# Attention row sums: ten of GpSimd's additions of the first diagonal tile replaced by accumulating transfers

## The chip, the cores and the metric

The kernel runs on one core of one Trainium2 chip. The metric is the device time of one execution in microseconds (us). Before the change it is 2240.48 us, the median of 3 runs (2238.31 to 2241.14). The profiled execution, from which every duration below comes, took 2238.97 us by the same clock, and 2237.2 us lie between its first and its last instruction. 0.2% of the time, about what a measurement of this kernel can tell from no change, is 4.5 us.

## The reference

One block of a transformer on two batch rows of 2048 tokens with 512 features: adaptive layer norm, causal attention with 16 heads of 32 features, a projection with a gate, then a feed-forward layer of 2048 hidden features. Everything is float32. The change touches the attention alone:

```python
scores = jnp.einsum('bhqd,bhkd->bhqk', q, k) * scale
causal = jnp.tril(jnp.ones((t, t), bool))
scores = jnp.where(causal, scores, -jnp.inf)
attn = jax.nn.softmax(scores, axis=-1)
out = jnp.einsum('bhqk,bhkd->bhqd', attn, v)
```

The kernel computes the softmax as unnormalised exponentials, their products with the values, and the sums of the exponentials over the keys; the division by the sums comes later, in another stage.

## The kernel before, in words

**Units and steps.** The attention of a batch row (`attention_phase`) goes through 16 units, numbered u = 0 to 15. A unit (c, i) is a chunk c of four heads and a block i of 512 queries; the order of i is 0, 1, 2, 3 for c = 0 and 0, 2, 1, 3 for the other chunks. So units 2, 5, 9 and 13 have i = 2, and units 3, 7, 11 and 15 have i = 3. A unit takes 4i + 3 steps. Each of the first 4i steps handles one tile of 128 keys that all 512 queries see. The last three are diagonal: step 4i, here called **d**, has the first diagonal tile, again 512 queries wide; d+1 packs the second and the fourth diagonal tile together; d+2 has the third. The next unit's steps follow at once, as d+3, d+4 and so on. What a unit leaves over is done by a list of pending work that is flushed at a later step (`flush`).

**One step** (`scores_t`, lines 634 to 696): TensorE writes four PSUM banks, one a head. The first matmuls of a step put the negated row maxima into all four banks (`st<-fold,sel`, line 659), then one matmul a head adds the scores (`st<-qst,kst`, line 668). ScalarE takes the exponential of each bank into an SBUF tile `e` of 128 x 4 x 512 (line 675). There are four such tiles in rotation (`E_BUFS`, line 77), so the exponentials of step n+4 overwrite those of step n. There are four `st` banks, so the first matmuls of a step need the exponentials of the step before to be done with their banks. GpSimd zeroes the masked triangle of the diagonal tiles (`affine_select`, line 687): once for step d, twice for d+1, once for d+2. In the same step TensorE also makes some score products for the maxima of units up to three ahead (`s<-kst,qst`, `row.score`; a bank of the `st` kind may be lent, `st<-kst,qst`).

**Values and sums.** Two steps later (`LAG`) TensorE multiplies `e` with the values into the bank `o` (line 715). The sums over the keys need a matmul with ones as well (`row_sums`, line 836, bank `sm`). To save those matmuls, GpSimd first adds the `e` tiles of four full steps into one tile `ee`, called a chain (lines 698 to 711, recorded at line 700: three additions of 128 x 2048 elements), and TensorE sums the chain once. In units with i of 2 or 3, GpSimd also adds the `e` tile of step d onto the chain of the last group, at step d+1 (line 844), after the three selects of d and d+1. The chain is then summed at the flush of step d+4 (lines 869 and 870), together with the other two diagonal tiles, which TensorE sums directly. `ee` has two buffers (line 78). At the end of a unit ScalarE copies `o` and `sm` into SBUF tiles `ot` and `sums` (lines 737 and 743, two buffers each), and SyncE stores them.

**What orders the work.** The order of the instructions on each engine is the program's own (`keep_in_program_order`, lines 205 to 215). All loads and stores of the attention are issued by SyncE (SP), in order. At the start of unit u it issues the four query loads of unit u+3 (line 780; four tiles in rotation, so they wait until unit u-1 is through with its queries, which is during its step d+2). At the start of units 4 and 8 it also loads the keys of the next chunk (line 783). Unit 12 reads the sums of units 0 to 11 back (`inverses`, line 398).

Of the kernel before, what the change touches and what calls it, by code (L numbers as in the profile page):

```python
# [8 lines left out]
F32 = mybir.dt.float32  # L9
# [3 lines left out]
ALU = mybir.AluOpType  # L13
# [4 lines left out]
P = 128  # L18
# [3 lines left out]
QB = 512  # L22
# [5 lines left out]
def dit_block_kernel(  # L28
# [36 lines left out]
    nc = tc.nc  # L65
# [9 lines left out]
    NG = T // MT  # L75
    LAG = 2
    E_BUFS = 4
    EE_BUFS = 2
    AHEAD = 3

    const = ctx.enter_context(tc.tile_pool(name="const", bufs=1))
# [89 lines left out]
    n_early = (C - 1) * NQ  # L171
# [37 lines left out]
    def act(ins):  # L209

        return tc.keep_in_program_order(ins)
# [412 lines left out]
    def attention_phase(row):  # L624
        b, vv, kst, qst = row.b, row.vv, row.kst, row.qst
        row.paced = True
        with pool(f"att{b}") as ap, pool(
# [70 lines left out]
            def add(u, dst, x, y):  # L698
                if u < len(units) - 1:
                    act(nc.gpsimd.tensor_tensor(dst, x, y, ALU.add))  # L700
                    return
                for h in range(HC):
                    act(nc.vector.tensor_tensor(dst[:, h], x[:, h], y[:, h], ALU.add))

            def add_to(u, chain, es):
                add(u, chain, chain, es)

            def begin_chain(u, es0, es1):
                chain = ap.tile([P, HC, QB], F32, tag="ee", name="ee", bufs=EE_BUFS)
                add(u, chain, es0, es1)  # L710
                return chain

            def products(dst, lhs, es, q0, at, first, last):
                for h in range(HC):
# [2 lines left out]
                        es[:, h, at : at + QB - q0], start=first, stop=last,  # L717
                    )

            def begin_diagonal(es0, es1):  # L720
                chain = ap.tile([P, HC, QB], F32, tag="ee", name="ee", bufs=EE_BUFS)
                act(nc.gpsimd.tensor_copy(chain[:, :, :P], es0[:, :, :P]))
                act(
                    nc.gpsimd.tensor_tensor(
                        chain[:, :, P:], es0[:, :, P:], es1[:, :, : QB - P], ALU.add
                    )
                )
                return chain
# [5 lines left out]
            def finish(u, o):  # L734

                c, i = units[u]
                ot = ap.tile([P, QB], F32, tag="ot", name="ot", bufs=2)
                act(nc.scalar.copy(ot, o))
                nc.sync.dma_start(od[b][i][:, c, :], ot)

            def finish_sums(u, sm):

                sums = ap.tile([P, QB], F32, tag="sums", name="sums", bufs=2)
                act(nc.scalar.copy(sums, sm))
                nc.sync.dma_start(sums_d[b][u], sums[0:P:HD, :])

# [2 lines left out]
            now = 0  # L749

            def flush(upto):
                while pending and pending[0][0] <= upto:
                    pending.pop(0)[1]()
# [25 lines left out]
            for u, (c, i) in enumerate(units):  # L779
                if NQ <= u + AHEAD < len(units):  # L780
                    row.load_queries(u + AHEAD)
                if u % NQ == 0 and c + 1 < C:
                    row.load_keys(c + 1, 0, NG)
                steps = len(steps_of[u])
                for n_step, tiles in enumerate(steps_of[u]):
                    last = n_step == steps - 1
                    if n_step == 0:
                        summed = set()
                        o = ps_op.tile([P, QB], F32, tag="o", name="o")
                        sm = ps_op.tile([P, QB], F32, tag="sm", name="sm")  # L790
                    ready = row.at

                    n = row.count(
                        due(u, starts[u] + n_step) - QB // 2,
                        u + AHEAD - (n_step < 2 and u > 0),
                    )
                    if u == 0 and n_step < LAG:

                        n = max(n, HC)
                    es, rest = scores_t(u, n_step, n)  # L800
                    rest = len(row.todo) - rest
                    make_rows = False
                    if u + 1 < len(units) and row.rows_made == u + 1:
                        if last:
                            row.score(row.count(cum[-1], u + 1))
                    row.settle()
                    if u + 1 < len(units) and row.rows_made == u + 1:
                        make_rows = last or (ready > u + 1 and n_step >= 1)
                    row.inverses(u, n_step)
                    if u == len(units) - 1:  # L810
                        row.prepare(n_step)
                    if make_rows and not last:
                        row.rows(u + 1)
                    flush(now)
                    if make_rows and last:
                        row.rows(u + 1)
                    row.score(max(0, len(row.todo) - rest))
                    row.settle()

                    def tile_by_tile(dst, lhs, es, tiles, first, last):  # L820
                        at = 0
                        for n, (j, q) in enumerate(tiles):
                            products(
                                dst, lambda h: lhs(j, h), es, q, at,
                                first and n == 0, last and n == len(tiles) - 1,
                            )
                            at += QB - q

                    def values(es=es, tiles=tiles, c=c, o=o, first=n_step == 0, last=last):
                        tile_by_tile(  # L830
                            o,
                            lambda j, h: vv[:, j, (c * HC + h) * HD : (c * HC + h + 1) * HD],
                            es, tiles, first, last,
                        )

                    def row_sums(es, last, tiles=((0, 0),), sm=sm, summed=summed):
                        first = not summed
                        summed.add(len(summed))
                        tile_by_tile(sm, lambda j, h: ones[:, :HD], es, tiles, first, last)

                    pending.append((now + LAG, values))
                    sums_of, wait = None, 0
                    if i and n_step == i * TQ + 1:
                        add_to(u, chain, single)
                    if n_step < i * TQ:
                        k = n_step % TQ
                        if k == 0:
                            even = es
                        elif k == 1:
                            chain = begin_chain(u, even, es)  # L850
                        else:
                            add_to(u, chain, es)
                        if k == TQ - 1 and n_step + 1 < i * TQ:
                            sums_of, wait = (chain, False), 2
                    elif i < 2 and u < len(units) - 2:
                        if n_step == i * TQ:
                            single = es
                        elif not last:
                            pair = es
                            if i == 0:  # L860
                                chain = begin_diagonal(single, pair)
                        else:
                            if i:
                                add_tail(chain, pair, P, 0)
                            add_tail(chain, pair, 3 * P, 3 * P)
                            add_tail(chain, es, 2 * P, 0)
                            sums_of, wait = (chain, True), 2
                    elif i and n_step == i * TQ:
                        single = es
                        sums_of, wait = (chain, False), 2  # L870
                    else:

                        sums_of, wait = (es, last, tiles), i > 0 and not last
                    if sums_of:
                        pending.append(
                            (now + LAG + wait, lambda f=row_sums, s=sums_of: f(*s))
                        )
                    if last:
                        pending.append((now + LAG, lambda u=u, o=o: finish(u, o)))
                        pending.append(  # L880
                            (now + LAG + wait, lambda u=u, sm=sm: finish_sums(u, sm))
                        )
                    pending.sort(key=lambda p: p[0])
                    now += 1
# [482 lines left out]
    with pool("wada") as wp, pool("qkv0") as qp, pool("hl0") as hp, pool(  # L1367
# [160 lines left out]
        pieces.done()  # L1528

    attention_phase(row)  # L1530


# [67 lines left out]
    with ExitStack() as mlp:  # L1600
# [7 lines left out]
        sums = [  # L1608
            wp.tile([P, 2 * MT], F32, tag=f"sum{n}", name=f"sum{n}") for n in range(4)
        ]  # L1610
# [926 lines left out]
```

## Time and profile before

| | us |
|---|---|
| median of 3 runs | 2240.48 |
| the profiled execution | 2238.97 |
| its span | 2237.2 |
| TensorE busy in the span | 2196.1 |
| GpSimd busy in the span | 1458.9 |
| attention of the first batch row | about 205 to 715 |
| attention of the second batch row | about 950 to 1455 |

PE is TensorE's matmuls, PEld its weight loads, DVE VectorE, ACT ScalarE, POOL GpSimd and SPq the sequencer that issues SyncE's transfers. A row of the view in order of time has start, duration, engine, line, operation, output and inputs, how many instructions were merged, and in brackets the idle time before it with the instruction that ended it. A row of the windows has for each engine its busy time and number of instructions, then the granted clock of TensorE, the busy share of the 16 DMA engines and the rate that they moved.

### The profile page before, as it was taken

Reading aid. Unit: us, or ns where it says so; the run is one execution under the profiler, and the core shown is the slowest. Engines: PE = TensorE matmul, PEld = TensorE weight load, DVE = VectorE, ACT = ScalarE, POOL = GpSimd, SP = SyncE. Lnnn points to the kernel's source line nnn. Section 1 sums busy time; section 2 is a strip of 40 time slices with the busy share of each in tenths; the row PEclk is TensorE's granted clock in tenths of the full one; section 3 lists DMA queues with packets and bytes.
Section 4 is the critical chain, followed back from the end, with each engine's and each line's share of the span. In section 5 each row is a group of like instructions: output and inputs, shape, how many; then the busy total and the mean of one; then the engine's idle time right before and its main releaser. Section 6 shows DMA issues by size and latency. Waiting matters only on the chain.

```text
span 2237.2 us, 34305 instructions
## 1 busy us (share of the span) xinstructions
PE 2196.1 (98%) x12273; PEld 1470.9 (66%) x12273; DVE 1580.7 (71%) x3373; ACT 1038.0 (46%) x2132; POOL 1458.9 (65%) x903
## 2 busy tenths in 40 slices
PE   7999999999999999999999999999999999999998
PEld 5887555555543588855555555345788888888887
DVE  4578766767757676777677777656586687688587
ACT  4444555655555244355655555703323532532520
POOL 4253998998992696189989898456616616535540
PEclk9999999999999999999999999999999999999999
DMA  8787143232233799542324113376655554654653
GB/s 273 249 278 192 42 89 76 67 86 48 88 111 114 258 311 317 153 105 62 86 67 104 35 52 127 105 243 216 236 181 177 192 173 157 212 183 142 219 158 111
DMA packets 166627, 340.99 MB, mean 152 GB/s; under 512 B 17216, under 2 KB 49516, under 8 KB 164664
## 3 DMA queue, kind: packets, MB, share of 16 engines
q1 hardware_dynamic: 158080, 302.05, 45.0%
q0 software_dynamic: 8000, 36.21, 4.3%
q8 instruction: 97, 1.59, 0.3%
q14 instruction: 74, 0.61, 0.1%
q10 hardware_dynamic: 376, 0.55, 0.1%
HBM read 246.46 MB, written 100.14 MB: 155 GB/s over the span
## 4 chain that ended last, share of the span: by engine, by line
PE 88%; DVE 4%; POOL 3%; DMA 2%; ACT 1%; issue 1%; SPq 0%; DVEq 0%; ACTq 0%; POOLq 0%
PE ps_a L207 23%; PE st L207 18%; PE ps_b L207 14%; PE o L207 10%; PE s L207 9%; PE ps_c L207 4%; PE ps_o L207 4%; PE sm L207 3%; DVE junk L503 1%; POOL ee L700 1%; PE ps_xt L215 1%; ACT e L675 1%; DVE mx L509 1%; PE ps_o L215 1%; POOL wqk L949 0%
## 5 line engine op out<-in xcount | busy, mean ns | idle before, releaser
L675 ACT ACTIVATE e<-st 128x512 f32<-128x512 f32 (+1 forms) x1152 | 574.7, 578 | 363.4 <-PE st L207 317.5
L509 DVE TENSOR_REDUCE mx<-s 128x1 f32<-128x512 f32 x576 | 381.7, 686 | 193.9 <-PE s L207 192.9
L700 POOL TENSOR_TENSOR ee<-ee,e 128x2048 f32<-128x2048 f32 x106 | 485.9, 4584 | 10.2 <-ACT e L675 4.3
L207 PE MATMUL st<-qst,kst 128*128 128x512 f32 (+3 forms) x1280 | 408.8, 386 | 0.0
L207 PE MATMUL s<-kst,qst 128*128 128x512 f32 (+3 forms) x1046 | 380.6, 395 | 6.0 <-DVE mx L509 3.7
L207 PE MATMUL ps_a<-sum,w 128*128 128x256 f32 (+1 forms) x1304 | 335.6, 391 | 3.1 <-DVE sum L1637 2.9
L207 PE MATMUL o<-e,vv 128*32 128x512 f32 (+3 forms) x2560 | 293.2, 537 | 0.3 <-POOL e L687 0.3
L207 PEld LDWEIGHTS st<-qst,kst 128*128 128x128 f32 x1280 | 228.5, 188 | 97.5 <-issue 65.7
L207 PEld LDWEIGHTS ps_a<-sum,w 128*128 128x128 f32 x1304 | 246.2, 190 | 44.3 <-issue 6.6
L503 DVE CUSTOM_DVE_ANT_0 junk<-s,causal 128x128 bf16<-128x128 f32 (+3 forms) x470 | 220.8, 470 | 61.2 <-PE s L207 47.4
L207 PEld LDWEIGHTS s<-kst,qst 128*128 128x128 f32 x1046 | 194.9, 188 | 71.0 <-DVE mx L509 17.0
L700 POOL TENSOR_TENSOR ee<-e 128x2048 f32<-128x2048 f32 x42 | 192.5, 4584 | 43.0 <-ACT e L675 43.0
L207 PE MATMUL ps_b<-sum,w 128*128 128x256 f32 (+1 forms) x744 | 186.8, 382 | 0.0
L2228 POOL TENSOR_TENSOR h<-h,h 128x512 f32<-128x512 f32 x96 | 119.4, 1274 | 69.8 <-DVE h L1734 69.8
L207 PEld LDWEIGHTS <-sel 32*128 32x128 bf16 x1152 | 29.6, 91 | 197.5 <-issue 196.6
L207 PEld LDWEIGHTS ps_b<-sum,w 128*128 128x128 f32 x744 | 140.4, 190 | 22.5 <-issue 2.6
L509 DVE TENSOR_REDUCE mx<-st 128x1 f32<-128x512 f32 x192 | 131.1, 683 | 0.5
L687 POOL TENSOR_SCALAR_AFFINE_SELECT e<-e 128x512 f32<-128x512 f32 x128 | 83.2, 669 | 68.1 <-ACT e L675 68.1
L1799 POOL TENSOR_TENSOR sum<-xm 128x256 f32<-128x256 f32 x22 | 23.2, 1054 | 154.3 <-PE ps_a L207 154.3
L207 PEld LDWEIGHTS o<-e,vv 128*32 128x32 f32 x2560 | 59.1, 108 | 92.3 <-issue 73.2
L207 PE MATMUL st<-fold,sel 32*128 32x512 bf16 (+1 forms) x1152 | 117.7, 372 | 1.4
L1071 POOL TENSOR_TENSOR lo<-lo,hi 128x512 fp32r<-128x512 f32 x32 | 40.7, 1274 | 105.7 <-ACT hi L1069 100.7
(263 smaller groups left out, 3580.4 us busy)
## 6 DMA issues: line engine op xcount, KB each, us to landing
w<-w1x SPq DMA_DIRECT2D x42, 896.0 KB
qst<-q SPq DMA_DIRECT2D x128, 256.0 KB
kst<-k SPq DMA_DIRECT2D x128, 256.0 KB
w<-w2d SPq DMA_DIRECT2D x28, 1024.0 KB
w<-w2d SPq DMA_DIRECT2D x28, 768.0 KB
q<-hi SPq DMA_DIRECT2D x32, 256.0 KB
q<-lo SPq DMA_DIRECT2D x32, 256.0 KB
k<-hi SPq DMA_DIRECT2D x32, 256.0 KB
```

What stands on the lines that cost most here:

```text
L207: return tc.keep_in_program_order(nc.tensor.matmul(*args, **kw))
L215: return tc.keep_in_program_order(nc.tensor.transpose(dst, src, ident[:n, :n]))
L503: nc.vector.tensor_tensor_reduce(junk[:, :w], x, causal[:, QB - w :], 1.0, MASKED, ALU.add, ALU.max, m,)
L509: self.vector(nc.vector.tensor_reduce(m, x, axis=AX.X, op=ALU.max))
L675: act(nc.scalar.activation(e4[:, h, :w], sts[h][:, :w], AF.Exp))
L687: nc.gpsimd.affine_select(d, d, pattern=[[0, HC], [1, P]], compare_op=ALU.is_ge, fill=0.0, base=0, channel_multiplier=-1,)
L700: act(nc.gpsimd.tensor_tensor(dst, x, y, ALU.add))
L1071: engine.tensor_tensor(lo, d, hi.bitcast(F32), ALU.subtract)
L1799: act(engine.tensor_tensor(dst, u, v, ALU.subtract))
L2228: act(engine.tensor_tensor(d[j], d[j], x[j], ALU.add))
```

## The change

In units 2, 3, 5, 7 and 9 of each batch row (`joined`: i of 2 or 3, and u below 11), the `e` tile of step d is no longer added onto the chain by a GpSimd instruction. GpSimd issues one DMA of 128 x 2048 floats instead, from `e` in SBUF onto `ee` in SBUF, with an addition as accumulating operation. It stands at the same place in GpSimd's order. The sum of that chain, and with it the end of the unit's sums and their copy and store, moves from the flush of step d+4 to that of d+6 (`JOIN_LAG`). `ee` gets three buffers, `ot` and `sums` one each. Units 11, 13 and 15 are as before.

```diff
-    EE_BUFS = 2
+    EE_BUFS = 3
+    JOIN_LAG = 2
...
+            def join(chain, es):
+                act(nc.gpsimd.dma_start(chain, es, accum_op=ALU.add))
...
-                ot = ap.tile([P, QB], F32, tag="ot", name="ot", bufs=2)
+                ot = ap.tile([P, QB], F32, tag="ot", name="ot", bufs=1)
...
-                sums = ap.tile([P, QB], F32, tag="sums", name="sums", bufs=2)
+                sums = ap.tile([P, QB], F32, tag="sums", name="sums", bufs=1)
...
+                    joined = i >= 2 and u < n_early - 1
                     if i and n_step == i * TQ + 1:
-                        add_to(u, chain, single)
+                        if joined:
+                            join(chain, single)
+                        else:
+                            add_to(u, chain, single)
...
-                        sums_of, wait = (chain, False), 2
+                        sums_of, wait = (chain, joined), 2 + JOIN_LAG * joined
                     else:
 
-                        sums_of, wait = (es, last, tiles), i > 0 and not last
+                        sums_of, wait = (es, last and not joined, tiles), i > 0 and not last
...
-                            (now + LAG + wait, lambda u=u, sm=sm: finish_sums(u, sm))
+                            (
+                                now + LAG + wait + JOIN_LAG * joined,
+                                lambda u=u, sm=sm: finish_sums(u, sm),
+                            )
```

## The prediction

> **What bounds the kernel now.** The first page says where the whole span goes: TensorE is busy 98% of it, and the chain of work that ended last runs through TensorE for 88% and through GpSimd for 3%. GpSimd has many additions of 4.58 us, and these are what the change takes a few of.
>
> ```profile
> span 2237.2 us, 34305 instructions
> PE 2196.1 (98%) x12273; PEld 1470.9 (66%) x12273; DVE 1580.7 (71%) x3373; ACT 1038.0 (46%) x2132; POOL 1458.9 (65%) x903
> PE 88%; DVE 4%; POOL 3%; DMA 2%; ACT 1%; issue 1%; SPq 0%; DVEq 0%; ACTq 0%; POOLq 0%
> L700 POOL TENSOR_TENSOR ee<-ee,e 128x2048 f32<-128x2048 f32 x106 | 485.9, 4584 | 10.2 <-ACT e L675 4.3
> ```
>
> An average over all stages doesn't say what bounds the attention, so next come the windows of its two rows, and the view of the exponentials' line, which lists what ScalarE waited for.
>
> ```profile
> 200.00:715.00 515.00, 508.65 (x3514) 260.98 (x3513) 371.17 (x900) 305.50 (x610) 439.43 (x170) 1.00 0.33 85
> 945.00:1455.00 510.00, 504.34 (x3476) 259.04 (x3475) 369.45 (x899) 304.31 (x607) 434.51 (x166) 1.00 0.32 85
> ```
>
> ```profile
>   POOL ee L700: 29.7, 22
> ```
>
> In 515 us TensorE idles 6.4 us, and in 510 us it idles 5.7 us. So TensorE alone sets the pace of both stages, at full clock. GpSimd is nearly as full (439 of 515), and ScalarE does wait for it 22 times, 29.7 us in all; but TensorE's own idle time, for all reasons together, is less than half of that in the two rows, so most of it doesn't reach TensorE. Whatever the change frees on GpSimd can give back at most the 12.0 us in which TensorE stands still, and what it makes later costs full price once it reaches TensorE.
>
> **What the change removes.** Ten additions of 4.58 us leave GpSimd. TensorE's instructions stay the same in number: ten groups of `sm<-ee` move two steps later, past matmuls that are done anyway.
>
> What waits for the removed addition? The exponentials of step d+4 overwrite the `e` tile of step d, so they need its last reader to be done. The view in order of time shows unit 2: GpSimd ends three selects and starts the addition at 279.13, and ScalarE starts the exponentials of d+4 as soon as it ends. The other four additions of this batch row follow, then the first exponential of d+4 in unit 5, where ScalarE was released by TensorE and not by GpSimd.
>
> ```profile
> 277.35 1.80 POOL L687 TENSOR_SCALAR_AFFINE_SELECT e<-e 128x512 f32<-128x512 f32 x3
> 279.13 4.57 POOL L700 TENSOR_TENSOR ee<-ee,e 128x2048 f32<-128x2048 f32 x1
> 331.64 4.56 POOL L700 TENSOR_TENSOR ee<-ee,e 128x2048 f32<-128x2048 f32 x1
> 379.85 4.59 POOL L700 TENSOR_TENSOR ee<-ee,e 128x2048 f32<-128x2048 f32 x1
> 462.16 4.58 POOL L700 TENSOR_TENSOR ee<-ee,e 128x2048 f32<-128x2048 f32 x1
> 510.21 4.58 POOL L700 TENSOR_TENSOR ee<-ee,e 128x2048 f32<-128x2048 f32 x1
> ```
>
> ```profile
> 283.73 2.06 ACT L675 ACTIVATE e<-st 128x512 f32<-128x512 f32 x4 [1.47 <-POOL ee L700]
> 386.79 0.60 ACT L675 ACTIVATE e<-st 128x512 f32<-128x512 f32 x1 [1.39 <-PE st L207]
> ```
>
> In the changed kernel the last reader is the transfer, and the exponentials of d+4 wait for its landing. **That is the wait put in place of the one removed**, and its length decides.
>
> **How late the landing may be.** Behind the waiting exponential on ScalarE stand the rest of that step and all that follow; TensorE waits for them when it starts step d+5, since its first matmuls write the four `st` banks that these exponentials free. TensorE's rows in order of time give the end of d+4 in unit 2, then the start of d+5 in all five units:
>
> ```profile
> 285.32 1.06 PE L207 MATMUL sm<-ee,ones 128*32 128x512 f32 x8
> 286.20 1.05 PE L207 MATMUL sm<-e,ones 128*32 128x384 f32 x16
> ...
> 288.04 0.40 PE L207 MATMUL st<-fold,sel 32*128 32x512 bf16 x4
> 339.77 0.29 PE L207 MATMUL st<-fold,sel 32*128 32x256 bf16 x4
> 390.92 0.40 PE L207 MATMUL st<-fold,sel 32*128 32x512 bf16 x4
> 470.36 0.29 PE L207 MATMUL st<-fold,sel 32*128 32x256 bf16 x4
> 521.33 0.40 PE L207 MATMUL st<-fold,sel 32*128 32x512 bf16 x4
> ```
>
> The sum over the chain (286.20 - 285.32 = 0.88 us) leaves d+4, so d+5 can start 0.88 us sooner. Four exponentials take 2.06 us. From the moment at which GpSimd comes to the transfer, the landing may take, without any cost:
>
> - unit 2: 288.04 - 279.13 - 0.88 - 2.06 = 5.97 us
> - unit 3: 339.77 - 331.64 - 2.94 = 5.19 us
> - unit 5: 390.92 - 379.85 - 2.94 = 8.13 us
> - unit 7: 470.36 - 462.16 - 2.94 = 5.26 us
> - unit 9: 521.33 - 510.21 - 2.94 = 8.18 us
>
> These allowances sum to 32.73 us. The second batch row runs the same program; its unit 2 has 1032.82 - 1023.85 = 8.97 where the first has 8.91, so I count the first row twice. What a landing takes beyond its allowance stops TensorE, and TensorE has no slack to win it back.
>
> ```profile
> 1023.85 4.58 POOL L700 TENSOR_TENSOR ee<-ee,e 128x2048 f32<-128x2048 f32 x1
> 1032.82 0.40 PE L207 MATMUL st<-fold,sel 32*128 32x512 bf16 x4
> ```
>
> **How long the landing takes.** No accumulating transfer and none from SBUF to SBUF is in this trace. The nearest rows are GpSimd's plain stores of 896 KB from 128 partitions in the first stage: the issue in order of time, the issues and queue of the window 103 to 112, those of 125 to 143, and the line's summary.
>
> ```profile
> 103.48 0.58 POOL L1274 DMA_DIRECT2D w1d<-kst  x1 [0.30 <-POOL kst L1258]
> ```
>
> ```profile
> q0 software_dynamic: 288, 1.84, 49.6%
> ...
> w1d<-kst POOLq DMA_DIRECT2D x1, 896.0 KB, 3.9
> ```
>
> ```profile
> w1d<-kst POOLq DMA_DIRECT2D x1, 896.0 KB, 9.3
> w1d<-qst POOLq DMA_DIRECT2D x1, 896.0 KB, 9.9
> ```
>
> ```profile
> DMA to landing us min/median/max: 3.9/4.9/9.9
> ```
>
> An issue holds GpSimd for 0.58 us after 0.30 us of waiting, against 4.58 us. Two stores took 49.6% of 9 us on the 16 engines, so one takes 2.23 us of each engine, and of a landing of 3.9 us some 1.65 us are issue, first packet and completion. For 1024 KB the engines need 2.23 x 1024/896 = 2.55 us if adding costs them nothing, and 5.10 us if they fetch two streams, the tile and the sum. The landing, counted from GpSimd's arrival, then takes 0.30 + 1.65 + 2.55 = **4.5 us**, or 0.30 + 1.65 + 5.10 = **7.05 us**, with the engines free.
>
> They aren't free. Each of the five places falls on the query loads, which SP issues when the same step is through; in units 3 and 7 the keys follow:
>
> ```profile
> 331.39 1.91 SPq L365 DMA_DIRECT2D qst<-q  x4
> ```
>
> ```profile
> q1 hardware_dynamic: 576, 1.05, 79.4%
> ```
>
> ```profile
> 331.00:347.00 16.00, 15.68 (x142) 7.94 (x141) 5.37 (x11) 9.80 (x22) 14.80 (x12) 1.00 0.91 204
> 461.00:478.00 17.00, 17.00 (x150) 9.14 (x149) 10.31 (x27) 9.81 (x22) 15.76 (x13) 1.00 0.88 195
> ```
>
> The queue's row is that of 279 to 285, unit 2: the loads take 79.4% of 6 us, 4.76 us of every engine. A transfer that shares the engines with them lands between 0 and 4.76 us later; in units 3 and 7, where the engines are 91% and 88% busy for 16 us, at most 5.10 us later, if the queues take turns evenly. I take half of 4.76 for all five, so 7.05 + 2.38 = **9.4 us**, which lies between the two kinds of row for 896 KB, 3.9 and 9.9. The ends stay for the range: 4.5 us below; above, the worst store's 9.9 - 2.23 of overhead with two streams, 0.30 + 7.67 + 5.10 = 13.1 us.
>
> The Trainium skill bears on both halves, and the sum needs neither place. "DMA: Bandwidth & Descriptors", section "Anatomy of one DMA — SWDGE (gpsimd) path", fits a GpSimd transfer as 2.0 us plus bytes over 436 GB/s; for 1 MB that is an estimate of 4.4 us, by which the change costs nothing. The quiet store (3.9 us for 896 KB) agrees, those of 9.3 and 9.9 us do not. The section "Rules for kernel authors" of that page says that an accumulating transfer reads its destination and writes it later, which speaks for two streams and 9.2 us of cost before any sharing; no run here shows it yet.
>
> **The sum.** At 9.4 us the landings overrun by 3.43, 4.21, 1.27, 4.14 and 1.22 us, 14.3 us a batch row and 28.5 us for both: 2238.97 + 28.5 = 2267.5. The median before is 1.5 us above the profiled execution, so the forecast is **2268 us**.
>
> What I cost at nothing, with its cover:
>
> - GpSimd's freed time, 10 x (4.58 - 0.88) = 37 us, is not on TensorE's path; the next addition waits for an exponential of d+4 anyway.
> - The moved sums wait for the landing only at d+6, two steps behind the stall above, so they add nothing under some 13 us.
> - Query loads slowed by the transfer: a score matmul with new queries stands in d+5 of unit 3. They could come up to 5.10 us later, the transfer's share, against the 4.21 us that TensorE stands there already: 0 to 0.9 us in units 3 and 7, at most 3.6 us in all.
> - `ot` with one buffer: the closest two copies are stored 10.2 us apart, in the unit with three steps. Without that cover a copy would wait for a 256 KB store, at most the 9.9 us of the 896 KB one. `sums` has the same spacing, and the third `ee` buffer only removes waits.
>
> ```profile
> 340.58 0.47 PE L207 MATMUL s<-kst,qst 128*128 128x512 f32 x1 [0.20 <-issue]
> ```
>
> ```profile
> 340.09 0.34 SPq L739 DMA_DIRECT2D o<-ot  x1
> 350.32 0.34 SPq L739 DMA_DIRECT2D o<-ot  x1
> ```
>
> **The rivals.**
>
> - **Hidden.** The engines add in passing and the loads hardly disturb: landing in 4.5 us, under the smallest allowance of 5.19. Nothing stops, 2239 us. For it: the stores of 3.9 us. Against it: five places out of five fall on busy engines. Up to 6.2 us the cost stays under 4.5 us (2 x (0.23 + 1.01 + 0.94) = 4.4).
> - **Much slower.** Each landing takes 13.1 us or more: 5 x 13.1 - 32.73 = 32.8 a row, 2305 us. For it: the stores of 9.3 and 9.9 us, and that adding could cost more than fetching twice.
> - **Faster: ScalarE is let go sooner.** Where the landing beats the addition, under 4.58 us, the waits in front of d+4 shrink: 1.47 us in unit 2 and at most as much in unit 3, 5.9 us in both rows if all of it reached TensorE, 2233 us. The point of decision is a landing of under 4.58 us together with TensorE held up at d+5. Against it: ScalarE ends the exponentials of unit 2 at 285.79 and TensorE wants the banks at 288.04, so that wait is not felt today.
>
> **How the numbers follow.** Forecast (landing 6.2 to 12 us, 2243.5 to 2293.5): 0.57. Hidden: 0.20. Much slower: 0.17. Faster: 0.06. The range goes from 2239, which takes in hidden, to 2304, the bound of 13.1 us; beyond it are faster and some 0.1 of much slower. Faster by over 0.2%: 0.06; within 0.2%, which is 4.5 us and about what a measurement of this kernel can tell: 0.20; slower: 0.74.
>
> **What would show it.** In the changed profile ten DMA issues of under 1 us on GpSimd with their landing times; ScalarE's first exponential of d+4 released by that DMA; TensorE idle before `st<-fold,sel` of d+5 by the landing less the allowance, most in units 3 and 7; as many matmuls as before. The forecast is wrong if the landings are under 6.2 us, if idle time shows elsewhere (the loads of queries, the sums at d+6, copies waiting for stores), or if step d+5 starts late without such a landing.

## The result, and the profile after

| | before | after |
|---|---|---|
| median of 4 runs each, us | 2239.77 | 2294.65 |
| lowest to highest | 2238.31 to 2241.14 | 2292.58 to 2300.93 |
| the profiled execution | 2238.97 | 2295.03 |

The change costs 54.9 us; the ratio on record is 1.0257, with a 95% interval of 1.0244 to 1.0269 (the two medians alone give 1.0245). The sign and the range of the prediction hold, but the cost is nearly twice the forecast 28.5 us.

The first page of the changed kernel answers to the lines shown of before:

```profile
span 2293.3 us, 34336 instructions
PE 2211.7 (96%) x12273; PEld 1476.2 (64%) x12273; DVE 1583.5 (69%) x3373; ACT 1038.5 (45%) x2132; POOL 1418.8 (62%) x903
PE 76%; POOL 10%; DMA 6%; DVE 4%; ACT 2%; issue 2%; SPq 0%; ACTq 0%; DVEq 0%; POOLq 0%
L701 POOL TENSOR_TENSOR ee<-ee,e 128x2048 f32<-128x2048 f32 x96 | 440.2, 4585 | 10.1 <-ACT e L676 3.8
```

GpSimd did lose its ten additions (x106 to x96, 1458.9 to 1418.8 us), and the chain shows where that went: TensorE's share falls from 88% to 76%, the rest is mostly GpSimd and DMA, for which TensorE now waits. The matmuls are as many as before, x12273. So TensorE's row gives the account of the whole loss in two terms. Its idle time is 2293.3 - 2211.7 = 81.6 us against 2237.2 - 2196.1 = 41.1, which is **40.5 us more standing still**. And the same matmuls are busy 2211.7 - 2196.1 = **15.6 us longer**. The second term is not in the prediction.

The windows of the two attention rows show both (their times are later than before, since the rows got longer):

```profile
206.00:745.00 539.00, 511.48 (x3495) 260.91 (x3494) 368.56 (x886) 305.28 (x609) 419.95 (x169) 0.98 0.35 89
980.00:1510.00 530.00, 507.55 (x3455) 258.94 (x3455) 365.98 (x885) 303.80 (x606) 414.91 (x165) 0.98 0.35 88
```

TensorE idles 27.5 and 22.5 us where it idled 6.4 and 5.7, and the granted clock is 0.98 where it was 1.00.

The wait itself is the predicted one. The view of the transfer's line, in the changed kernel:

```profile
L722 POOL DMA_DIRECT2D ee<-e x10: 821/856/882, 280.2 to 1309.3; - x10
  ACT e L676: 59.5, 10
DMA to landing us min/median/max: 8.4/9.6/13.2
```

All ten times ScalarE's exponentials wait for the landing, 59.5 us in all. The instructions in order of time, first unit 2 (GpSimd's selects and its issue, ScalarE, then TensorE), then TensorE's stops in units 3, 5 and 7 of the first row:

```profile
278.45 1.82 POOL L688 TENSOR_SCALAR_AFFINE_SELECT e<-e 128x512 f32<-128x512 f32 x3
280.21 0.88 POOL L722 DMA_DIRECT2D ee<-e  x1
...
291.94 2.06 ACT L676 ACTIVATE e<-st 128x512 f32<-128x512 f32 x4 [8.50 <-DMA ee<-e]
...
292.59 0.80 PE L208 MATMUL st<-kst,qst 128*128 128x512 f32 x1 [6.73 <-ACT e L676]
...
293.99 1.93 PE L208 MATMUL sm<-e,ones 128*32 128x384 f32 x16
...
354.18 1.83 PE L208 MATMUL st<-fold,sel 32*128 32x256 bf16 x4 [5.58 <-ACT e L676]
...
407.32 0.51 PE L208 MATMUL st<-kst,qst 128*128 128x512 f32 x1 [1.24 <-ACT e L676]
...
495.75 1.83 PE L208 MATMUL st<-fold,sel 32*128 32x256 bf16 x4 [6.55 <-ACT e L676]
```

Read the rows of unit 2 as one chain: the transfer is issued at 280.21, straight behind the selects, ScalarE may go on at 291.94, TensorE stands for 6.73 us until 292.59. And then the row at 293.99: those 16 matmuls take 1.93 us, and the same 16 took 1.05 us before (286.20 in the prediction). The windows of the changed kernel say why; the column behind GpSimd's is the granted clock:

```profile
285.00:293.00 8.00, 1.27 (x5) 0.78 (x4) 1.27 (x3) 1.06 (x3) 0.00 (x0) 0.75 0.74 154
293.00:297.00 4.00, 4.00 (x40) 1.89 (x39) 2.20 (x6) 1.56 (x4) 2.91 (x1) 0.65 0.00 0
297.00:301.00 4.00, 4.00 (x27) 2.17 (x24) 2.48 (x4) 2.10 (x5) 2.78 (x2) 1.00 0.17 66
```

The clock goes to one half during the stop and stays there for 6.8 us, past the end of the stop. The trace has six such stretches in the attention, each of 6.8 us, one at each of units 2, 3 and 7 of both rows, and none at units 5 and 9; before had none. In them TensorE works for 3.2, 6.1 and 4.5 us in the first row and 4.7, 4.7 and 6.4 us in the second, 29.6 us in all. At half clock that is work of 14.8 us, so the clock accounts for 14.8 of the 15.6 us of longer matmuls.

Last, the DMA queues of the changed kernel. q0 carries GpSimd's transfer, q1 SyncE's loads. In unit 2 the windows are 280 to 284 and 284 to 292, in unit 5, where GpSimd issues at 398.09, 398 to 404 and 404 to 407:

```profile
q1 hardware_dynamic: 307, 0.58, 70.2%
...
q0 software_dynamic: 144, 1.05, 63.4%
q1 hardware_dynamic: 269, 0.47, 24.2%
```

```profile
q0 software_dynamic: 112, 0.92, 80.7%
...
q1 hardware_dynamic: 220, 0.41, 50.6%
q0 software_dynamic: 32, 0.13, 30.9%
```

In unit 2, for the four microseconds behind the issue, only the query loads move: no row of q0 stands in that window. Not all of this is waiting: in unit 5, where nothing is ahead of it, the first packet of the transfer leaves 1.4 us after the issue. There the loads are the ones that wait. SyncE issues them 1.4 us behind the transfer, and they have no row before 404:

```profile
399.52 4.24 SPq L366 DMA_DIRECT2D qst<-q  x4
```

So at these two places the two don't share the engines evenly; what is ahead is, for the most part, served first. Unit 7 is not so simple. The transfer is issued at 481.79 and lands at 495.00; the window is 480 to 496:

```profile
q1 hardware_dynamic: 1034, 1.90, 54.3%
q0 software_dynamic: 144, 1.05, 31.9%
```

54.3% of 16 us are 8.7 us of loads on each engine, at most one of them behind the landing. Four query loads are some 4.76 us (unit 2 before), so key loads that SyncE issued behind the transfer moved between its packets too.

### The profile page after: what moved, and what is told of

The parts are those of the page before. It is cut to its first block, busy times and chain, and to the rows that moved or that the text cites. A ratio compares the mean times of both kernels' runs of the same rounds, so it can differ in the third digit from the quotient of the medians.

```text
span 2293.3 us, 34336 instructions
## 1 busy us (share of the span) xinstructions
PE 2211.7 (96%) x12273; PEld 1476.2 (64%) x12273; DVE 1583.5 (69%) x3373; ACT 1038.5 (45%) x2132; POOL 1418.8 (62%) x903
## 4 chain that ended last, share of the span: by engine, by line
PE 76%; POOL 10%; DMA 6%; DVE 4%; ACT 2%; issue 2%; SPq 0%; ACTq 0%; DVEq 0%; POOLq 0%
PE ps_a L208 22%; PE ps_b L208 13%; PE st L208 13%; PE o L208 7%; POOL ee L701 7%; PE s L208 7%; PE ps_o L208 4%; DMA ee<-e 4%; PE ps_c L208 4%; PE sm L208 3%; ACT e L676 2%; DVE junk L504 1%; PE ps_xt L216 1%; POOL e L688 1%; POOL ee L736 1%
## 5 line engine op out<-in xcount | busy, mean ns | idle before, releaser
L701 POOL TENSOR_TENSOR ee<-ee,e 128x2048 f32<-128x2048 f32 x96 | 440.2, 4585 | 10.1 <-ACT e L676 3.8
L208 PE MATMUL st<-kst,qst 128*128 128x512 f32 x234 | 96.1, 411 | 18.2 <-ACT e L676 18.2
```

The costliest lines, as they stand in the source:

```text
L208: return tc.keep_in_program_order(nc.tensor.matmul(*args, **kw))
```

## The experiments

My theory from these views: the cost is (a) the part of the landing beyond the allowance, (b) the half clock that follows a long stop, and the landing itself is two streams plus the loads queued ahead. Rivals: the other edits (moved sums, single buffers) cost it; an accumulating transfer is slow by nature, wherever it stands; each transfer has a fixed price; the slow matmuls don't come from the stops.

**The other edits alone.** Everything of the change but the transfer:

```diff
-                        if joined:
-                            join(chain, single)
-                        else:
-                            add_to(u, chain, single)
+                        add_to(u, chain, single)
```

> Everything of the change is kept (sums moved to d+6, three ee buffers, one ot and one sums buffer) but GpSimd's addition, which stands again in place of the transfer. If the transfer's landing is the whole cost: 2238 to 2242 us, as before, and no half-clock stretch. If the moved sums or the single buffers cost something: anything up to 2295, with idle time before the copies or the sums.

Measured: 2239.02 us (11 runs), before 2237.66 beside it, ratio 1.0006 (0.9997 to 1.0015). The moved sums, the third `ee` and the single `ot` and `sums` buffers cost nothing that can be told from noise.

**Neither addition nor transfer.**

```diff
-                        if joined:
-                            join(chain, single)
-                        else:
+                        if not joined:
                             add_to(u, chain, single)
```

> In the ten joined units neither the addition nor the transfer is made; the first diagonal tile's part of those units' sums is left out. This is what a transfer of no cost at all could reach. If GpSimd is off the path: 2236 to 2241. If an earlier release of ScalarE at d+4 is worth something, as the rival for faster had it: down to 2233.

Measured: 2240.77 us (11 runs), ratio 1.0011 (1.0002 to 1.002). Even a transfer that takes no time at all brings nothing: GpSimd's freed time is worth nothing here, and the rival for faster falls.

**The transfer without its addition.**

```diff
-                act(nc.gpsimd.dma_start(chain, es, accum_op=ALU.add))
+                act(nc.gpsimd.dma_start(chain, es))
```

> The transfer without its addition: it overwrites the chain with the first diagonal tile, so the last group's sum is left out in ten units. If a landing is two streams of engine time plus the queueing behind query loads: the time on an engine falls from 5.1 to about 2.6 us, the landings by 2.5 us to between 6 and 10, and the stops by 2.5 us in units 2, 3 and 7, with the half-clock stretches gone where the stop falls under some 2 to 3 us: 2250 to 2268. If the addition as such costs nothing and the queue alone counts: 2290 to 2295.

Measured: 2279.21 us (4 runs), ratio 1.0185 (1.017 to 1.0201): above what my theory had. Two windows of its trace show why, unit 2 (276 to 289) and unit 9 (531 to 540); the first row is unit 2 of the change (279 to 292):

```profile
q0 software_dynamic: 144, 1.05, 39.0%
...
q0 software_dynamic: 144, 1.05, 26.5%
ee<-e POOLq DMA_DIRECT2D x1, 1024.0 KB, 10.0
...
q0 software_dynamic: 144, 1.05, 34.7%
ee<-e POOLq DMA_DIRECT2D x1, 1024.0 KB, 5.4
```

Engine time falls, but less than to the 2.6 us expected: from 39.0% of 13 us = 5.07 to 26.5% of 13 us = 3.45 in unit 2, and to 34.7% of 9 us = 3.12 in unit 9. In unit 9 the landing follows (8.4 to 5.4 us, and the stop is gone). In unit 2 it falls by 1.6 us only, from 11.6 to 10.0, and in unit 7 from 13.2 to 12.9. So the adding adds to the work of the transfer, but in units 2, 3 and 7 much of the landing is not the transfer's own work.

**Only units 5 and 9.** `joined = u in (5, 9)`.

> Only units 5 and 9 of each row use the transfer; units 2, 3 and 7 keep GpSimd's addition. If the cost is the landing beyond the allowance: four stops of 1.1 to 1.2 us and no half clock, 2239.8 + 4.9 = 2244 to 2246. If each transfer has one fixed price wherever it stands (54.9 / 10 = 5.5 us): 2262.

Measured: 2243.21 us (7 runs), 5.6 us above the 2237.66 beside it, ratio 1.0027 (1.0016 to 1.0038). Four stops, all of this form and 1.21 to 1.23 us long:

```profile
387.62 0.50 PE L208 MATMUL st<-kst,qst 128*128 128x512 f32 x1 [1.23 <-ACT e L676]
```

They sum to 4.9 us and the clock stays at full. A fixed price per transfer (22 us for four) is out: the place decides.

**The transfer in a quiet place.** The kernel before, with the third addition of three groups of unit 11 done by three kinds of transfer:

```diff
+                        elif u == 11 and k == TQ - 1:
+                            (quiet_add, quiet_copy, quiet_half)[n_step // TQ](chain, es)
```

> The kernel before, with three additions of unit 11 replaced where no load of queries or keys runs: one accumulating transfer of 1 MB, one plain copy of 1 MB, one accumulating transfer of 512 KB (the copy and the half leave part of two sums out). If two streams and the queueing behind query loads make up the landing: 7.0 to 8.5 us for the first, as in units 5 and 9 where it was served first (8.4), about 5.4 for the copy and about 5 for the half, with packets of 628 ns, 311 and 314. If an accumulating transfer is slow by itself: 10 us or more for the first.

Measured: 2236.81 us (one run). The windows 556 to 563 (accumulating, 1 MB) and 567 to 573 (plain copy):

```profile
q0 software_dynamic: 128, 1.05, 73.8%
ee<-e POOLq DMA_DIRECT2D x1, 1024.0 KB, 7.0
...
q0 software_dynamic: 144, 1.05, 45.3%
ee<-e POOLq DMA_DIRECT2D x1, 1024.0 KB, 4.5
```

Alone, the accumulating transfer lands in 7.0 us with 73.8% of 7 us = 5.17 us of each engine; the copy in 4.5 us with 2.72 us, so here the adding nearly doubles the work; half the size, accumulating, in 4.5 to 4.7 us. A transfer that is slow by nature (10 us or more) is out.

**Five e buffers.** `E_BUFS = 5` and `EE_BUFS = 2`, the rest as changed.

> The changed kernel with five e buffers and two ee: the e tile of step d is overwritten at d+5 instead of d+4, which gives the landing one more step (3.4 us in most). If the landing beyond the allowance is the cost: the stops fall to some 3.3, 2.2 and 3.2 us in units 2, 3 and 7, to none in 5 and 9, and most half-clock stretches go: 2250 to 2265. If the transfer costs by loading SBUF or the queues, whoever waits: 2290 to 2295.

Measured: 2272.44 us (4 runs), ratio 1.0153 (1.0138 to 1.0168). Down by 22 us from the change, as a landing beyond an allowance must, but short of what I expected. Unit 2 stops for 2.40 us (3.3 expected) and units 5 and 9 not at all. Unit 3 stops at another place, SyncE's row first, then TensorE's:

```profile
335.62 1.91 SPq L366 DMA_DIRECT2D qst<-q  x4
...
350.52 0.76 PE L208 MATMUL s<-kst,qst 128*128 128x512 f32 x1 [6.78 <-issue]
```

This is the first score with the new queries. It starts 14.90 us after their loads were issued, and before the change 9.19 us after (340.58 - 331.39, both rows in the prediction). This row names no releaser, but in the second batch row the same matmul stops for 5.75 us (at 1113.56), and there the row names the query load, `DMA qst<-q`. If it is the loads here too, the transfer delays them by at least 5.7 us, since before the change that matmul had hardly waited (0.20 us). TensorE, no longer held up in d+4, runs straight into them: 6.78 and 5.42 us in units 3 and 7 of the first row, 5.75 and 3.84 us in those of the second. A second wait of much the same size had stood hidden behind the first.

**The clock.** The changed kernel, with useless matmuls into a free bank ahead of the six long stops:

```diff
+    FILL = ({2: 26, 3: 21, 7: 25}, {2: 26, 3: 8, 7: 14})
...
+                fill = FILL[b].get(u - 1, 0) if step == 1 else 0
+                if fill:
+                    s = ps_sp.tile([P, QB], F32, tag="s", name="fill")
+                    for _ in range(fill):
+                        mm(s, kst[c, 0][:, 0, :P], qst[u][:, 0, :], start=True, stop=True)
```

> The changed kernel with extra matmuls of no use into a free bank, written ahead of the six places where TensorE stands long, as many as fill the stop. If the half clock follows from TensorE's standing still: the clock stays at 1.00 through units 2, 3 and 7 and the time falls by what the slow matmuls cost, 15 us, to about 2280. If the slow stretches come from something else (power, the transfer itself): they stay, and the time is 2295 or, by the extra matmuls, a little more.

Measured: 2287.89 us (4 runs, 2282.87 to 2293.79), ratio 1.0222 (1.0199 to 1.0245), 6.8 us less than the median of the change and short of the 2280 expected. The profiled execution is the fastest of the four, 2282.87, which is 12.2 us less than the profiled one of the change. In it five of the six slow stretches are gone, while the landings are no shorter (10.4 us on average against 10.15). Unit 2 with its fill, then a window behind it, then one behind unit 3 of the second row, where the landing came later than the fill reached and TensorE still stood for 2.79 us:

```profile
281.93 6.19 PE L209 MATMUL fill<-qst,kst 128*128 128x512 f32 x26
...
289.25 0.51 PE L209 MATMUL st<-kst,qst 128*128 128x512 f32 x1 [1.14 <-ACT e L677]
```

```profile
291.00:295.00 4.00, 4.00 (x41) 2.00 (x32) 3.02 (x7) 2.65 (x5) 4.00 (x1) 1.00 0.19 70
...
1116.00:1120.00 4.00, 3.61 (x15) 2.08 (x17) 1.33 (x2) 3.00 (x8) 2.79 (x4) 0.50 0.93 212
```

TensorE did more work and the kernel got faster: the slow matmuls come from the standing still. The other runs, which have no trace, go the same way: 2283.93 at a mean clock of 0.999, and 2291.86 and 2293.79 at 0.995 and 0.996, where the fill seems to have missed some stops.

**Loads two steps later, first try.** The call of the query and key loads was moved from the start of the unit behind a joined one to its third step, and the score products of the new queries were allowed two steps later.

```diff
-                if NQ <= u + AHEAD < len(units):
-                    row.load_queries(u + AHEAD)
-                if u % NQ == 0 and c + 1 < C:
-                    row.load_keys(c + 1, 0, NG)
+                late = 2 * (0 < u < n_early and units[u - 1][1] >= 2)
...
+                    if n_step == late:
+                        if NQ <= u + AHEAD < len(units):
+                            row.load_queries(u + AHEAD)
+                        if u % NQ == 0 and c + 1 < C:
+                            row.load_keys(c + 1, 0, NG)
...
-                        u + AHEAD - (n_step < 2 and u > 0),
+                        u + AHEAD - (n_step < 2 + late and u > 0),
```

> The changed kernel with the query and key loads that follow a joined unit issued two steps later, and the score products of the new queries allowed two steps later too. If the queue ahead of it is what makes a landing 11.5 to 13.5 us in units 2, 3 and 7: all landings come to 8.4 to 8.8 as in units 5 and 9, the stops to 2.7, 3.5 and 3.4 us in units 2, 3 and 7, some half-clock stretches go, and the time is 2262 to 2275, plus what late queries cost. If the landing depends on the step or the buffers and not on the loads: it stays at 2290 to 2295.

Measured: 2305.62 us (4 runs), ratio 1.0301 (1.0283 to 1.0318), landings of 8.4 to 11.7 us. In units 2 of both rows this tells nothing: the loads went out as early as before, since nothing but a free query buffer held them on SyncE, and the landings stay at 11.0 and 11.7 us. In unit 7 of both rows the loads did come later, 1.2 us behind the transfer, and its landing falls from 13.2 to 9.9 us and from 10.4 to 9.1 us, which speaks for the loads.

**Loads two steps later, held.** As above, and the late query loads as well as the store of `ot` are kept in the program's order, so that SyncE issues the queries behind that store:

```diff
+                if held:
+                    act(load())
...
-                nc.sync.dma_start(od[b][i][:, c, :], ot)
+                act(nc.sync.dma_start(od[b][i][:, c, :], ot))
```

> The edit that the run before it missed (there SyncE issued the loads as early as ever, since nothing held them): now the query and key loads after a joined unit stand behind that unit's store of o on SyncE, so they go out after step d+4, when the transfer has landed. If the loads ahead of it in the queues make the landing long: 7 to 8.5 us in all five units, stops of 1.3 to 2.7, 2.1 to 3.5 and 2.0 to 3.4 us in units 2, 3 and 7, the half clock gone in most; what the late queries cost comes on top, and the landings, not the time, decide. If a landing is long in these units for another reason: 11 to 13 us as before.

Measured: 2302.41 us (4 runs), ratio 1.0289 (1.0272 to 1.0306). The landings in the first row, unit 2 (window 278 to 289) and unit 5 (396 to 406):

```profile
q0 software_dynamic: 144, 1.05, 47.3%
...
ee<-e POOLq DMA_DIRECT2D x1, 1024.0 KB, 7.4
```

```profile
q0 software_dynamic: 144, 1.05, 51.8%
...
ee<-e POOLq DMA_DIRECT2D x1, 1024.0 KB, 6.9
```

No row of q1 stands in either window, and the landing falls from 11.6 to 7.4 us in unit 2 and from 8.5 to 6.9 in unit 5 (second row: 6.9 and 7.1), about the 7.0 of the quiet place. Same step, same buffers, same transfer: the loads in the queues were what made it long. Units 5 and 9 no longer stop. In units 3 and 7 it stays at 8.6 to 11.5 us; loads on q1 still ran there, the last keys of the chunk among them, and I haven't split these up further. The time doesn't fall, because late queries cost about as much as the late landing did. TensorE stops for them four times, 4.87 to 6.20 us each; the first is in unit 3:

```profile
359.19 0.77 PE L208 MATMUL s<-kst,qst 128*128 128x512 f32 x1 [4.87 <-DMA qst<-q]
```

Its idle time is that of the change, 2300.4 - 2220.6 = 79.8 us against 81.6. The half clock isn't gone, as I had expected, but lasts longer (mean clock 0.985 against 0.990), and TensorE is busy 8.9 us longer than in the change.

**Two units, five e buffers.** `joined = u in (5, 9)`, `E_BUFS = 5`, `EE_BUFS = 2`.

> Only units 5 and 9 use the transfer, and with five e buffers (two ee) their exponentials wait a step later: the landing of 8.4 us then lies inside the allowance. If only a landing beyond the allowance costs: no stop in units 5 and 9 and 2237 to 2241 us, equal to before. If a transfer costs something even when nobody waits for it (slower loads, SBUF): above 2242.

Measured: 2237.51 us (11 runs), ratio 0.9999 (0.999 to 1.0008).

```profile
DMA to landing us min/median/max: 8.4/8.5/8.6
```

The landings are as long as in the change and nobody waits for them: a transfer that lands inside its allowance costs nothing, and brings nothing. With the run that left the additions out altogether, this says that taking these ten additions off GpSimd can't beat the kernel before, however the transfer is placed.

## Why the prediction came out as it did

**What bounds the kernel: right.** TensorE sets the pace; GpSimd's relief is worth nothing in the two runs that isolate it: with all ten additions left out GpSimd is busy 1410.3 us and not 1458.9, and the ratio is 1.0011; with two units and five buffers, where nobody waits for the four transfers, it is busy 1442.4 us, and the ratio is 0.9999.

**The wait put in place: right.** ScalarE waits for the landing ten times out of ten, and TensorE behind it. The other edits cost nothing (1.0006).

**The allowances: right in sum.** With the measured landings they give overruns of 5.66, 7.01, 0.35, 7.95 and 0.21 us in the first row and 5.55, 3.61, 0.30, 5.11 and 0.26 in the second, 36.0 us. At the same ten places TensorE stops for ScalarE's exponentials for 6.73, 5.58, 1.24, 6.55 and 1.14 us in the first row and 6.69, 2.41, 1.19, 3.93 and 1.19 in the second, 36.7 us. One by one they are rougher. In units 2, 5 and 9 TensorE stops before the end of d+4, at a score into a lent bank (`st<-kst,qst`, the rows at 292.59 and 407.32), which I hadn't counted: 1.24 us of stop in unit 5 for 0.35 of overrun. In units 3 and 7 the first matmul of d+5 needs one bank and not all four: 5.58 for 7.01. That the two errors cancel in the sum is luck.

**Two streams: right.** 7.05 us with the engines free was counted from 0.30 us ahead of the issue, so 6.75 from it; the quiet place gave 7.0, with 5.17 us of engine time against the estimate of 5.10. (The 9.2 us of cost "before any sharing" is a slip: with 7.05 us the allowances give 2 x (1.08 + 1.86 + 1.79) = 9.5.) The Trainium skill, "DMA: Bandwidth & Descriptors", section "Anatomy of one DMA — SWDGE (gpsimd) path", gave an estimate of 4.4 us for 1 MB: the quiet plain copy agrees (4.5), the accumulating transfer doesn't (7.0). Its section "Rules for kernel authors", by which such a transfer reads its destination first, agrees with 5.17 us of engine time against 2.72.

**The step that failed: "I take half of 4.76 for all five, so 7.05 + 2.38 = 9.4 us".** The wait behind the loads is neither half of them nor the same at all five places. In units 5 and 9 the transfer is ahead and lands in 8.4 to 8.5 us, 1.4 to 1.5 more than the 7.0 of the quiet place, and the loads pay. In units 2, 3 and 7 the loads are ahead, and it lands in 8.8 to 13.2 us, 1.8 to 6.2 more. The mean is 10.15 us, so the loads cost 3.15 where the prediction has 2.38. The 0.30 us ahead of the issue, taken over from the row of a store, didn't occur: at all ten places GpSimd goes to the issue without a gap, as in unit 2 (the selects end at 280.27). So a landing takes 10.15 us from GpSimd's arrival. That is only 0.75 us above the forecast, but ten times over it makes 36.0 - 28.5 = 7.5 us. The held loads, which brought the landing down to 7.4 us, and the plain copy, which lost only 1.6 us in unit 2, show the cause for units 2, 5 and 9. For units 3 and 7, where keys follow the queries, the split between what is ahead and what moves in between stays open.

**The term that was missing: the clock.** The prediction priced a stop at its own length, so it put the clock at nothing. The six stops of 2.19 to 6.73 us also halve the clock for the next matmuls, 15.6 us in all; filling the stops gave 12.2 of it back in the profiled execution, with one of the six stretches left, and 6.8 between the medians. The whole, between the two spans: 36.7 of stops at the ten places (28.5 forecast) + 1.8 of one late query load + 2.0 of idle time that I can't place + 15.6 of clock = 56.1, against 54.9 between the medians. The Trainium skill, "TensorE: Matmul & The Clock Gate", section "Part 1: The HAM clock gate", watches TensorE in windows of about 3.4 us, and its rule is that no idle gap be longer than that. The trace agrees for 6.73 us (clock 0.65 right behind it) and for 1.24 us (1.00), but in unit 3 of the second row a stop of 2.19 us was followed by half clock as well, so here the shorter one is the safer bound (the row of the stop, then the window behind it and the one behind the stop of 1.24 us):

```profile
1124.84 0.26 PE L208 MATMUL st<-fold,sel 32*128 32x256 bf16 x1 [2.19 <-ACT e L676]
```

```profile
1125.00:1129.00 4.00, 1.71 (x5) 0.52 (x4) 0.00 (x0) 2.12 (x5) 2.68 (x4) 0.53 1.01 208
406.00:410.00 4.00, 2.76 (x39) 1.29 (x38) 1.77 (x3) 2.50 (x5) 1.18 (x1) 1.00 1.02 224
```

The other runs show no sharp bound. In the attention every stop of 2.19 us or more was followed by half clock, and stops of 2.02 us (held loads) and 2.04 us (filled) were not; but in the held loads a stop of 0.62 us with three gaps of 0.23 us behind it was (at 1265.15).

**What was costed at nothing.** Freed time, moved sums and single buffers: right. The slowed query loads: the 5.10 us were near the 5.7 or more of the run with five buffers, and the cover (TensorE standing anyway) held in most places; in unit 3 of the second row the loads cost 1.82 us of their own. But the cover is the stall itself: with five e buffers it went, and the loads took its place with 6.78 us.

**The rivals.** Hidden and faster are out: the shortest landing is 8.4 us. Much slower named a time near the measured one (2305), but its mechanism, 13.1 us at every place, happened at one place in ten. The measured time came near it through the 15.6 us of the clock, which that rival doesn't have, so its nearness is luck.

## What to carry to other kernels

An operation moved from an engine to a DMA has two prices: the relief, which is nothing if the engine isn't the bound, and the latency, which must fit between the last write of its source and the next use of the buffer. For that latency, count everything that is issued in the same few microseconds ahead of it in full and not by half; here the loads cost it 1.8 to 6.2 us, and it is the cautious guess. Ask as well which loads it will stand ahead of. And a stop of TensorE above some two microseconds cost more than its length here, because the matmuls behind it ran at half clock.

## What the runs showed of the hardware that was not expected

- An accumulating transfer of 1 MB within SBUF takes 5.17 us of each DMA engine and lands in 7.0 us where nothing else runs; a plain copy of the same takes 2.72 us and lands in 4.5.
- Its issue holds GpSimd for 0.82 to 0.92 us, that of the plain copy for 0.56 to 0.61.
- GpSimd's queue and SyncE's queue were not served evenly. With the query loads issued 0.9 us ahead (unit 2), the first packet of the transfer left 4.0 us after its issue and not 1.4; with the transfer 1.4 us ahead (unit 5), the loads had no packet for 4.5 us. In unit 7 loads that were issued behind the transfer moved between its packets.
- In the changed kernel the clock was at one half for 6.8 us at each stop of 2.19 to 6.73 us, 3.2 us or more of it after the stop; stops of 1.14 to 1.24 us left it alone.
